# A graph layer on one core: one group in three, not one in four, sends all five of its windows through picked sets

## The chip, the cores and the metric

The kernel runs on one core of a Trainium2 chip. The metric is the device time of one execution in microseconds (us), as the median of several runs. The kernel before takes 1719.61 us (three runs, 1719.46 to 1721.19).

## The reference

A graph network layer with two edge types, a residual and a layer norm: 12500 nodes of 128 features, 400000 edges sorted by target node.

```python
src, dst = (edge_index[0], edge_index[1])
Xs = X[src]
m_data = Xs @ W_data.T + b_data
m_ctrl = Xs @ W_control.T + b_control
msg = jnp.where((edge_types == 0)[:, None], m_data, m_ctrl)
agg = jax.ops.segment_sum(msg, dst, num_segments=X.shape[0])
out = agg + (X @ W_self.T + b_self)
return jax.nn.relu(out)
...
x = _layernorm(x + _L0_gnn_ref(...), axis=-1)
```

## The kernel before

**Groups, windows and chunks.** The edges are cut into 3125 chunks of 128, and these into 25 groups of 125. A group is five windows of 25 chunks. Because the edges are sorted by target, a window's edges go to a short run of nodes; a group has accumulators `acc` (feature by node, one for each edge type) and `cnt` (edge counts for the biases). Messages are summed before the weights are applied: the kernel adds up rows of x per target and type, and multiplies by W once per node when a group is finished.

x is held as three bf16 parts whose sum is the float32 number, 384 columns a row: in SBUF as `x3` (row n at block n // 128, lane n % 128), and in DRAM as `rows3`.

**Two ways for an edge to reach its source row.** A *gathered chunk* is an indirect DMA issued by POOL (`fetch`, L825): 128 rows of `rows3` arrive as the tile msg. PE then adds them into the window's PSUM bank with three matmuls (`add_rows`, L757), against a one-hot matrix psel (`choose`, L845, built by `select` at L533) with a column for each target node and type. A window's psel covers all its 25 chunks however many are gathered.

A *picked set* takes 20 chunks of a window at once and without a DMA per chunk. DVE ranks the 2560 edges by the block and lane of their source row (L597 to L676: O, prod, found, rank, rm, rv), PE sorts them into 100 cells of 32 (`put`, L688), a 0.8 MB broadcast DMA on SP's queue brings the cells' lanes to all partitions (`spread`, L699 and L701), DVE makes them one-hot (`pick_matrix`, L743), PE picks the rows out of x3 (`pick`, L926, into PSUM tiles got), ACT copies them out as emsg (L940), and PE sums them into PSUM against a one-hot matrix esel (L533, L757). Edges that don't fit their cell go to 64 spare places; every second set one indirect DMA on POOL fetches these for two sets (`spare_rows`, L901, tile both). ACT copies half of it for the later set (L988, tile last), which waits for that DMA.

`sets(g)` says how many of a group's five windows have a picked set: all five if g is a multiple of 4, else four. A window with a set gathers its other 5 chunks (PB); the fifth window of the other groups gathers all 25 (PL). That is 7 x 5 + 18 x 4 = 107 sets and 7 x 25 + 18 x 45 = 985 gathered chunks.

**The order of work.** The main loop (L1177) runs over the sets. In the turn of set w there stand its picking and summing (five units of five cell columns each, `picked`), the ranking of sets w + 2 and w + 3, the pick matrix of w + 1, the chunks due in this turn, and the group work: `prep` of the next group (loading of edges, turning them, L494 to L522), `finish` and `pass_on` of a group whose windows are all closed. Gathered chunks are spread evenly over the turns from the third on, by `at = LAG + (n + ...) * (pairs - LAG) / total` (L1160). Their DMAs are paced (`paced`, L830): up to eleven places in a turn may each issue one, when it is due, 14 chunks (AHEAD) before the chunk that is due there, gated by a PE instruction of that place. A both gather takes the next such place, and POOL's queue is served in order. There are 18 msg buffers (HOLD).

`near_rows` (L460) works out, for all groups at once, where each chunk's window begins; its last instruction of three covers the groups with five sets by a stride of 4 (L469).

Of the kernel before, what the change touches and what calls it, by code (L numbers as in the profile page):

```python
# [31 lines left out]
NE = 5  # L32
NWIN = 2 * NE
LAG = 2
DPC = P * N // E
PAD = 10
PW = DPC + 2 * PAD
EW = 88
AW = PW + DPC * (PL - 1)
WMAX = max(AW, EW)  # L40
# [11 lines left out]
AHEAD = 14  # L52
FAR = -(-PW // DPC)
ACC_ROWS = 99 * P
# [101 lines left out]
def row_tables(nc, keep, tmp):  # L156
# [22 lines left out]
    for v in range(2):  # L179
# [4 lines left out]
        from_p = from_of[:, v, 0:1]  # L184
        nc.vector.tensor_scalar(from_p, k, float(DPC), float(-PAD), op0=OP.mult, op1=OP.add)
        nc.vector.tensor_scalar(from_e, from_p, -1.0, -1.0, op0=OP.mult, op1=OP.add)
# [20 lines left out]
def short_path(ctx, tc, const, ident, eps, wT, brow, bad, x, src, dst, etype, ws, bs, out):  # L207
# [12 lines left out]
    def side():  # L220

        return ps1.tile([P, 512], FP, name="side")

    def windows(g):

        c = g * GC
        for i in range(NE):
            yield "p", i, c, PB
            yield "e", i, c + PB, EC
            c += PB + EC  # L230

    def sets(g):

        return NE if g % 4 == 0 else NE - 1

    def of_p(g, i):

        return PL if sets(g) < NE and i == NE - 1 else PB

    each_e = [(g, i) for g in range(NG) for i in range(sets(g))]  # L240
    raw = {}

# [151 lines left out]
    for i, (_, _, c, _) in enumerate(windows(0)):  # L394
        nc.vector.memset(least[:, :, i:i + 1], float(max(0, c * DPC - PAD)))
    nc.vector.memset(x3[:, NBLK - 1], 0.0)
# [63 lines left out]
    def near_rows():  # L460

        first = pre.tile([GC, NG], FP, name="first", bufs=1)
        nc.vector.tensor_copy(first, first_all)
        ps = side()
        for v in range(3):
            nc.tensor.matmul(
                ps[:GC, v * P:v * P + NG], pick_first[:GC, v, :], first, start=True, stop=True, skip_group_check=True
            )
        for v, k, each in ((2, 0, 1), (1, 1, 1), (0, 1, 4)):  # L469
            start = from_of[:GC, v % 2, k:k + 1]  # L470
            nc.vector.tensor_scalar(
                near_all[:, k, ::each], ps[:GC, v * P:v * P + NG:each], start, None, op0=OP.add
            )

    def prep(g):

        s, d, t = raw.pop(g)
        v = 0 if sets(g) == NE else 1
        width = bounds_of[:GC, v, 0:1]
        sf = pre.tile([GC, P], FP, name="sf", bufs=1)  # L480
# [369 lines left out]
    def count(ps, sel):  # L850

        for r in range(FAR):
            n = len(range(r, CHUNKS, FAR))
            at = 2 * AW + DPC * r
            for t in range(2):
# [301 lines left out]
    for p in range(NG * NE):  # L1157
        run = gathered(*divmod(p, NE))
        for k, (_, u) in enumerate(run):
            at = LAG + (n + 0.9 - k / len(run)) * (pairs - LAG) / total  # L1160
            chunks.setdefault(int(at), []).append((at % 1, u))
# [3 lines left out]

    due[:] = [(LAG - 0.1) * (k + 0.5) / AHEAD for k in range(AHEAD)] + due[:-AHEAD]

# [9 lines left out]
    for w in range(pairs):  # L1177
        g, i = each_e[w]
        more = [(0.5, lambda: later(near_rows))] if w == 0 else []
        first = 1 if g == 0 else 0  # L1180
        if i == first and g + 1 < NG:
# [179 lines left out]
```

## Time and profile before

| what | value |
|---|---|
| median of three runs | 1719.61 us |
| profiled execution | 1721.01 us, span 1719.3 us |
| granted TensorE clock | 0.994 |
| PE busy in the span | 1568.1 us |
| DVE busy | 1529.0 us |
| ACT busy | 1243.3 us |
| POOL busy | 1286.8 us |
| first pick of set 0, pick of the last set | 58.3 us, 1679.9 us |
| bytes moved by DMA | 248.30 MB |

Busy time of an engine is the union of its instructions in the profile, without issuing and semaphore instructions; PE is matmuls, PEld the weight loads that overlap them. A group row of the profile reads: line, engine, operation, tiles out<-in, shapes, count | busy us, mean ns | idle time of that engine just before these instructions, and what ended it. A row of the timeline gives start and duration in us; in brackets stands the idle time before it and who ended it.

### The profile page before, as it was taken

How to read it: one execution, taken by the hardware profiler on the slowest of the kernel's cores; microseconds unless marked ns; L12 is line 12 of the kernel's file. 1: busy time of each engine (PE TensorE's matmuls, PEld its weight loads, DVE VectorE, ACT ScalarE, POOL GpSimd, SP SyncE). 2: the span in 40 equal slices, each digit the busy share in tenths (PEclk: the TensorE clock that was granted, in tenths of full speed). 3: DMA queues.
4: the chain of work that ended last, by engine and by line, in shares of the span. 5: the costliest groups of instructions: out<-in, count | busy, mean ns of one | idle time of the engine just before them, and what ended most of it. 6: DMA issues, size and time to landing. Idle time of an engine off the chain costs nothing.

```text
span 1719.3 us, 68641 instructions
## 1 busy us (share of the span) xinstructions
PE 1568.1 (91%) x28525; PEld 1241.5 (72%) x28525; DVE 1529.0 (89%) x3630; ACT 1243.3 (72%) x2198; POOL 1286.8 (75%) x1061
## 2 busy tenths in 40 slices
PE   0599999999999999999899999999999999999997
PEld 0377777777777777777677777777777777777776
DVE  6899899998998989999799899999999899999983
ACT  5777677776777667777576777676777676777675
POOL 0288878888788888888788777777788787777872
PEclk9999999999999999999999999999999999999999
DMA  7844454545444454444445554545544445544442
GB/s 195 280 149 133 126 160 124 147 147 152 134 139 142 139 148 135 140 150 129 144 122 150 160 155 136 152 130 152 150 144 138 135 128 159 155 140 129 138 128 59
DMA packets 148973, 248.30 MB, mean 144 GB/s; under 512 B 35937, under 2 KB 115260, under 8 KB 148652
## 3 DMA queue, kind: packets, MB, share of 16 engines
q1 hardware_dynamic: 85994, 134.45, 23.6%
q0 software_dynamic: 50032, 102.98, 22.2%
q10 hardware_dynamic: 12626, 6.40, 1.4%
q8 instruction: 225, 3.69, 0.9%
q14 instruction: 96, 0.79, 0.1%
HBM read 226.24 MB, written 17.50 MB: 142 GB/s over the span
## 4 chain that ended last, share of the span: by engine, by line
DVE 40%; PE 38%; issue 8%; ACT 5%; DMA 4%; DVEq 1%; POOL 0%; SPq 0%; ACTq 0%; POOLq 0%
PE sums L757 16%; PE got L926 12%; DVE esel L533 5%; DVE prod L641 5%; DVE prod L636 4%; DVE rv L676 3%; DVE pick L743 3%; DVE found L643 3%; PE side L1045 3%; ACT emsg L940 2%; DVE prod L614 2%; PE side L624 2%; DMA both<-rows,idx 2%; DVE psel L533 2%; PE side L688 2%
## 5 line engine op out<-in xcount | busy, mean ns | idle before, releaser
L825 POOL DMA_INDIRECT msg<-rows,idx_g x985 | 1215.5, 1234 | 309.7 <-issue 143.8
L940 ACT CAST emsg<-got 128x768 bf16<-128x768 f32 (+1 forms) x1070 | 949.0, 931 | 296.9 <-PE got L926 277.8
L757 PE MATMUL sums<-esel,emsg 128*128 128x176 bf16 x7704 | 686.6, 240 | 3.4 <-DVE acc L814 2.9
L757 PEld LDWEIGHTS <-emsg 128*128 128x128 bf16 x7704 | 569.5, 98 | 106.1 <-issue 98.8
L926 PE MATMUL got<-x,pick 128*32 128x384 bf16 x10486 | 569.1, 330 | 17.9 <-ACT emsg L940 8.8
L926 PEld LDWEIGHTS <-pick 128*32 128x32 bf16 x10486 | 240.4, 96 | 143.8 <-issue 19.9
L533 DVE TENSOR_TENSOR esel<-code_col,code 128x1760 bf16<-128x1760 bf16 x321 | 292.9, 913 | 11.8 <-PE sums L757 8.8
L757 PE MATMUL sums<-psel,msg 128*128 128x48 bf16 x2955 | 167.2, 184 | 11.8 <-DVE acc L814 9.0
L757 PEld LDWEIGHTS <-msg 128*128 128x128 bf16 x2955 | 138.6, 97 | 21.2 <-issue 16.4
L641 DVE TENSOR_TENSOR prod<-prod 128x1200 bf16<-128x1200 bf16 x214 | 134.0, 626 | 7.2 <-issue 1.1
L533 DVE TENSOR_TENSOR O<-cell_col,blk 128x2000 bf16<-128x2000 bf16 x107 | 128.0, 1197 | 7.1 <-ACT blk L439 4.3
L636 DVE TENSOR_TENSOR prod<-O,ahead 128x2000 bf16<-128x2000 bf16 x107 | 128.3, 1200 | 4.5 <-DVE ahead L632 1.9
L743 DVE TENSOR_SCALAR pick<-pick,lane_f 128x3200 bf16<-128x3200 bf16 x107 | 112.9, 1055 | 0.1
L901 POOL DMA_INDIRECT both<-rows,idx x54 | 66.2, 1226 | 54.4 <-ACT emsg L940 41.8
L688 PE MATMUL side<-rv,O 128*128 128x64 bf16 x2140 | 83.4, 195 | 25.0 <-DVE rv L676 22.1
L533 DVE TENSOR_TENSOR psel<-near_col,near 128x1200 bf16<-128x1200 bf16 x125 | 96.7, 773 | 9.7 <-issue 8.7
L814 DVE TENSOR_TENSOR acc<-acc,sums 128x176 f32 (+2 forms) x232 | 66.8, 288 | 42.1 <-PE sums L757 41.3
L688 PEld LDWEIGHTS <-O 128*128 128x128 bf16 x2140 | 79.0, 100 | 27.2 <-DVE rv L676 22.3
L676 DVE TENSOR_TENSOR rv<-rm,vals 128x1280 bf16<-128x1280 bf16 x107 | 87.9, 822 | 3.3 <-DVE key L649 1.4
L643 DVE TENSOR_REDUCE found<-prod 128x20 f32<-128x600 bf16 x107 | 82.9, 775 | 3.2 <-DVE prod L641 0.4
L614 DVE TENSOR_TENSOR prod<-O 128x1000 bf16<-128x1000 bf16 x107 | 72.0, 673 | 0.0
L624 PEld LDWEIGHTS <-ltri 128*128 128x128 bf16 x1284 | 40.4, 96 | 40.0 <-issue 38.5
(196 smaller groups left out, 1544.6 us busy)
## 6 DMA issues: line engine op xcount, KB each, us to landing
pick<-there SPq DMA_DIRECT2D x106, 800.0 KB
msg<-rows,idx_g POOLq DMA_INDIRECT x985
acc<-acc_start SPq DMA_DIRECT2D x23, 640.0 KB
rows<-x SPq DMA_DIRECT2D x6, 1344.0 KB
xs<-in_x_dram SPq DMA_DIRECT2D x99, 62.5 KB
out_dram<-h SPq DMA_DIRECT2D x99, 62.5 KB
xt<-in_x_dram ACTq DMA_DIRECT2D x6, 896.0 KB
cnt<-cnt_start SPq DMA_DIRECT2D x22, 160.0 KB
```

The lines of the kernel that those rows point to most:

```text
L533: nc.vector.tensor_tensor(sel.rearrange("p n (w t) -> p n w t", t=2), col[:rows].rearrange("p (o w t) -> p o w t", o=1, t=2).to_broadcast( ...
L614: nc.vector.tensor_add(h[:, :2 * CQ], s["O"][:, :2 * CQ], s["O"][:, 2 * CQ:])
L636: nc.vector.tensor_tensor(prod[:, :, :NCELL], s["O"], ahead.rearrange("p (o j) -> p o j", o=1).to_broadcast([P, EC, NCELL]), op=OP.mult,)
L641: nc.vector.tensor_add(prod[:, :, :h], prod[:, :, :h], prod[:, :, h:2 * h])
L643: nc.vector.tensor_reduce(found, prod[:, :, :h], AX.X, OP.add)
L676: placed[:] = [nc.vector.tensor_tensor(rv.rearrange("p c v (r t) -> p c v r t", t=2), rm.rearrange("p c (o r t) -> p c o r t", o=1, t=2).t ...
L688: nc.tensor.matmul(s["rk"][:m, :2 * CAP], s["held"][:, c * NCELL:c * NCELL + m], s["rv"][:, c].rearrange("p v r -> p (v r)"), start=(c == ...
L743: nc.vector.tensor_scalar(t, t, lane_f, None, op0=OP.is_equal)
L757: last = nc.tensor.matmul(out, msg[:, j * D:(j + 1) * D], sel, start=(start and j == 0), stop=stop, skip_group_check=True)
L825: return nc.gpsimd.indirect_dma_start(out=msg, out_offset=None, in_=rows3[:, :], in_offset=bass.IndirectOffsetOnAxis(ap=codes["p", g][0][: ...
L926: last = nc.tensor.matmul(ps[CAP * a:CAP * (a + 1), :], slots[w]["pick"][:, a * NQ + q, :], x3[:, 4 * q + a - a0].rearrange("p j d -> p (j ...
L940: s["out"] = nc.scalar.copy(msg[:, :n], ps[:, :n, :3 * D])
```

## The change

A constant EACH = 3 takes the place of the 4, in `sets` and in the stride of `near_rows`. Groups 0, 3, 6, ..., 24 now have five sets: 9 x 5 + 16 x 4 = 109 sets, and 9 x 25 + 16 x 45 = 945 gathered chunks.

```diff
@@ -32,6 +32,7 @@
 NE = 5
 NWIN = 2 * NE
 LAG = 2
+EACH = 3
@@ -231,7 +232,7 @@
     def sets(g):
 
-        return NE if g % 4 == 0 else NE - 1
+        return NE if g % EACH == 0 else NE - 1
@@ -466,7 +467,7 @@
-        for v, k, each in ((2, 0, 1), (1, 1, 1), (0, 1, 4)):
+        for v, k, each in ((2, 0, 1), (1, 1, 1), (0, 1, EACH)):
             start = from_of[:GC, v % 2, k:k + 1]
             nc.vector.tensor_scalar(
                 near_all[:, k, ::each], ps[:GC, v * P:v * P + NG:each], start, None, op0=OP.add
```

All line numbers of the kernel after are one higher. POOL's queue, its first gathers of the main loop, before:

```order
L901 DMA both<-rows_115,idx 128x384
L825 DMA msg<-rows_115,idx_g 128x384 x17
L901 DMA both<-rows_115,idx 128x384
L825 DMA msg<-rows_115,idx_g 128x384 x18
L901 DMA both<-rows_115,idx 128x384
L825 DMA msg<-rows_115,idx_g 128x384 x19
```

The same places of the queue after (L902 is `spare_rows`, L826 is `fetch`; from one both to the next are two sets):

```order
L902 DMA both<-rows_115,idx 128x384
L826 DMA msg<-rows_115,idx_g 128x384 x16
L902 DMA both<-rows_115,idx 128x384
L826 DMA msg<-rows_115,idx_g 128x384 x18
L902 DMA both<-rows_115,idx 128x384
L826 DMA msg<-rows_115,idx_g 128x384 x18
```

Behind each both stands about one gather fewer, all through the program: 18 or 19 (20 at five places) before, 17 or 18 (19 at three) after.

DVE in the turn of set 17, which before is the first set of group 4, from the rank of set 19 on:

```order
L645 CAST rank<-found 128x40
L533 TENSOR_TENSOR rm<-rank_col,rank 128x640
L533 TENSOR_TENSOR esel<-code_col,code 128x1056
L676 TENSOR_TENSOR rv<-rm,vals_5777 128x1280
L494 TENSOR_SCALAR rel<-dsts,near_all 125x128 x2
L495 TENSOR_SCALAR kind_r<-typs 125x128
L499 TENSOR_TENSOR worst<-worst,rel 125x256
```

And after, where set 17 is the fifth set of group 3:

```order
L646 CAST rank<-found 128x40
L534 TENSOR_TENSOR rm<-rank_col,rank 128x640
L650 SCALAR_TENSOR_TENSOR key<-rank,pk 128x20
L677 TENSOR_TENSOR rv<-rm,vals_5747 128x1280
L615 TENSOR_TENSOR prod<-O 128x10x100
L605 TENSOR_TENSOR prod<-blk_6207,blk_184 128x20x20
```

A set more stands ahead of the preparation of group 5 (rel, kind_r, worst), which has moved to the next turn; the ranking of a set is the same run of instructions in both.

## Prediction

> **What bounds the kernel now.** First the page's busy line, then the groups of GpSimd.
>
> ```profile
> PE 1568.1 (91%) x28525; PEld 1241.5 (72%) x28525; DVE 1529.0 (89%) x3630; ACT 1243.3 (72%) x2198; POOL 1286.8 (75%) x1061
> ...
> L825 POOL DMA_INDIRECT msg<-rows,idx_g x985 | 1215.5, 1234 | 309.7 <-issue 143.8 <-PE got L926 61.5 <-PE sums L757 56.0
> ...
> L901 POOL DMA_INDIRECT both<-rows,idx x54 | 66.2, 1226 | 54.4 <-ACT emsg L940 41.8
> ```
>
> PE and DVE look like the bound, and POOL looks like an engine with a quarter to spare. The instructions of the tile msg (minimum, median and maximum in ns, first and last start; below, POOL's idle time by what ended it) say otherwise:
>
> ```profile
> L825 POOL DMA_INDIRECT msg<-rows,idx_g x985: 940/1092/4512, 77.5 to 1686.3; - x197
> ...
>   issue: 160.2, 503
>   PE got L926: 61.5, 179
>   PE sums L757: 56.0, 179
> ```
>
> Each gap is a constant: 160.2/503 = 0.32 us, 61.5/179 = 0.34, 56.0/179 = 0.31. POOL hardly ever waits for anything; it pays about 0.31 us to get from one gather to the next. So a gather occupies POOL for (1215.5 + 309.7)/985 = 1.55 us, and 985 of them, with 54 of the both gathers at about 1.53 us (1.226 and the same gap), make 1608 us, against 1686.3 - 77.5 = 1609 us from the first to the last gather. POOL's queue has no slack.
>
> That alone doesn't make POOL the bound, since gathers are paced up to 14 chunks ahead of their use. The place where it hurts shows in the timeline:
>
> ```profile
> 188.84 0.29 ACT L581 ACTIVATE idx<-part 128x1 int32<-128x1 f32 x1
> ...
> 198.25 1.67 POOL L901 DMA_INDIRECT both<-rows,idx  x1 [0.30 <-DMA msg<-rows,idx_g]
> ...
> 202.17 0.51 ACT L988 COPY last<-both 64x384 bf16<-64x384 bf16 x1 [4.09 <-DMA both<-rows,idx]
> 202.58 0.20 ACT L696 CAST cell<-side 128x64 bf16<-128x64 f32 x1
> ...
> 202.84 0.21 PE L709 MATMUL side<-ident_b,cell 128*32 128x25 bf16 x4 [3.48 <-ACT cell L696]
> ```
>
> The indices of a both gather were ready at 189.13, but it stood behind queued msg gathers until 198.25. ACT, in order, waited 4.09 us for its rows, and with ACT's next copy PE stood for 3.48 us. In the list of waits, and for two long stretches by themselves (the first row of the three is the whole run, the second the stretch 196.7 to 945.3, the third what ended idle time before the tile both's instructions in 945.3 to 1656.6):
>
> ```profile
> ACT last L988 <- DMA both<-rows,idx: 29.0, 16, 7.1
> ```
> ```profile
> ACT last L988 <- DMA both<-rows,idx: 22.2, 13, 7.1
> ```
> ```profile
>   DMA both<-rows,idx: 4.0, 1
> ```
>
> The two stretches, all engines, and then the picks (L743, one for each set) alone:
>
> ```profile
> core 0: us, PE busy (x) PEld busy (x) DVE busy (x) ACT busy (x) POOL busy (x), PEclk, DMA share, GB/s
> 196.70:945.30 748.60, 702.62 (x12810) 557.63 (x12810) 672.98 (x1571) 538.10 (x971) 600.24 (x477) 0.99 0.47 141
> 945.30:1656.60 711.30, 679.43 (x12521) 539.92 (x12519) 652.68 (x1520) 527.82 (x944) 558.95 (x464) 1.00 0.48 144
> ```
> ```profile
> 196.70:945.30 748.60, 50.76 (x48) 0.99 0.47 141
> 945.30:1656.60 711.30, 49.54 (x47) 1.00 0.48 144
> ```
>
> A set takes 15.60 us in the first, 15.13 in the second. With 0.305 us behind each of its 477 and 464 instructions POOL is taken to 99.6% and 98.5%. In the second stretch PE is busy for 95.5% and DVE for 91.8%, and only one both gather comes late. So PE and DVE together set the pace, and a full POOL queue adds stalls on top. The change moves work from the second kind of cost to the first.
>
> **The change, part by part.** Two sets are added. In the quiet stretch, less its one wait of 4.0, a set's time is (711.3 - 4.0)/47 = 15.05 us, which holds also the gathered chunks and the groups' work. Their PE rows there (msg by the tile, with PE, PEld and POOL; then three rows of the groups' work):
>
> ```profile
> 945.30:1656.60 711.30, 75.06 (x1329) 62.27 (x1329) 529.80 (x441) 1.00 0.48 144
> ```
> ```profile
> L856 PE MATMUL sums<-psel,one_col 128*32 128x96 bf16 (+1 forms) x636 | 25.1, 208 | 0.0
> L1045 PE MATMUL side<-wT,acc 128*125 128x128 f32 x160 | 24.0, 273 | 0.0
> ...
> L1045 PE MATMUL side<-wT,xT 128*125 128x128 f32 x80 | 18.2, 309 | 0.8
> ```
>
> Chunks take 75.06/47 = 1.60 us of a set's time, counting and finishing 67.3/47 = 1.43. A set by itself is 15.05 - 1.60 - 1.43 = 12.0 us, two are **+24.0**. Between what ends? With the 0.68 us in which PE idles per set filled, 11.3 each; if the set waits on DVE alone, so that chunks hide and nothing is taken off for them, 15.05 - 1.43 = 13.6. I take 12.0, the value of the stretch itself. The two sets' other parts (a 0.8 MB broadcast each on SP's queue, one more both gather, ten ACT copies each) lie beside this: ACT was busy for 527.82 of 711.3 and DMA for 0.48.
>
> Forty gathered chunks go. On PE a chunk is 75.06/443 (1329 matmuls, three each) = 0.17 us, together **-6.8**; if DVE is what is waited for, nothing. The one-hot psel of a window is built for all 25 of its chunks whichever path they take, so DVE saves nothing there. Counting stays whole too. Edits to the two indexing strides cost nothing that differs: the same three instructions write 9 columns instead of 7.
>
> On POOL 40 gathers go and one both comes: -40 x 1.55 + 1.53 = -60 us. Per set that is (945 x 1.55 + 55 x 1.53)/107 = 14.5 us where 15.3 stood, against the 15.0 that PE and DVE need: 96% taken, with 0.5 us a set to work a backlog off. What that buys is only the waits behind the queue. What is an ACT wait worth on PE's path? 3.48/4.09 = 0.85 at 202; the two stretches differ by 0.47 x 48 = 22 us, of which the first has two finished groups more (rows below, 50.6 against 42.2 us, so 8.4), and 14 us stand against 18.2 us more waiting, 0.77. With 0.85, 29.0 us are worth 24.7. At 98.5% taken 4.0 us were left of 22.2, so at 96% I take nine tenths as gone: **-22.2**. Bounds: nothing gone, or all 29.0.
>
> ```profile
> L1045 PE MATMUL side<-wT,acc 128*125 128x128 f32 x192 | 28.8, 273 | 0.0
> ...
> L1045 PE MATMUL side<-wT,xT 128*125 128x128 f32 x96 | 21.8, 308 | 1.0
> ```
>
> What is late next when those stalls go: PE's short waits for DVE and ACT within each set, which 12.0 includes. Sum: +24.0 - 6.8 - 22.2 = -5.0. The profiled execution took 1721.0 us (span 1719.3 and 1.7 around it), so 1716.0; the median of the runs is 1.4 lower than it, so **1714.6, said as 1715**.
>
> **Rivals.** *Even trade.* The price of the sets at 20 and a relief of 20 cancel: 1719.6. Two terms of one size with opposite signs make this the nearest neighbour of the forecast. Nothing within 0.2% (3.4 us) can be told from no change.
>
> *The backlog stays, slower.* Gathers are stretched by DVE, as here, where one took 4.51 us (940 ns is the least):
>
> ```profile
> 559.93 4.51 POOL L825 DMA_INDIRECT msg<-rows,idx_g  x1 [0.30 <-issue]
> 559.94 1.18 DVE L533 TENSOR_TENSOR O<-cell_col,blk 128x2000 bf16<-128x2000 bf16 x1
> ...
> 561.05 1.19 DVE L636 TENSOR_TENSOR prod<-O,ahead 128x2000 bf16<-128x2000 bf16 x1
> ...
> 562.16 0.77 DVE L533 TENSOR_TENSOR psel<-near_col,near 128x1200 bf16<-128x1200 bf16 x1
> ...
> 562.85 1.28 DVE L641 TENSOR_TENSOR prod<-prod 128x1200 bf16<-128x1200 bf16 x2
> ...
> 564.34 0.78 DVE L643 TENSOR_REDUCE found<-prod 128x20 f32<-128x600 bf16 x1 [0.21 <-DVE prod L641]
> ```
>
> Two more sets bring more DVE instructions of this kind. The stretch is 1.234 - 0.940 = 0.29 us a gather, 290 us in all, 2.7 us a set. If it belongs to the set, it falls on 8.8 instead of 9.4 gathers: 1.247 us each. POOL stays full from the point at which 17.7 gathers and one both fill two sets' 30.0 us: a mean of (30.0 - 1.53)/17.7 - 0.305 = 1.30 us. Then only some 5 us of waiting go, and +17.2 - 5 = +12 gives 1732; with the sets at 13.6 and no relief from chunks, +27 - 5, it is 1741. Against it stands that 1.247 is short of 1.30. The Trainium skill's page "SBUF — State Buffer", section "Who interferes with whom", says that a tensor_tensor takes only the shared read interface and infers that it does not hold up descriptor generation, while a tensor_scalar in a two-port mode blocks GpSimd for its whole length. By that rule only the pick of a set (1.06 us, 50.76/48) and small ones count against the change. The 4.51 us gather lay beside a run of tensor_tensors with no tensor_scalar among them, so this trace speaks against the inference.
>
> *POOL is the clock.* If PE's 91% are not PE at its peak and POOL's gapless queue alone sets the end, the time falls with it. With the stretch kept to the sets: -40 x (0.940 + 0.31) + 2 x 2.7 + 1.2 = -43, so 1676. Against it: the second stretch ran 3% faster per set than the first with the same POOL queue, and -43 would ask for 14.6 us a set from a PE that now leaves 0.68 of 15.13 idle. The Trainium skill, "Trainium Kernel Development and Optimization", section "Performance Expectations", calls matmul busy time a bad metric, because matmuls are pipelined, and weight loads' busy share a good one. By that rule PE, with loads at 72%, has room and this rival gains. The rows of stalls, where PE stands idle for an ACT that waits, are too few to carry 43 us.
>
> *The change does not do what it says* can be left out: the written order has 945 and 55 gathers.
>
> **How the numbers follow.** Forecast, 1700 to 1716: 0.42. Even trade, within 3.4 us of 1719.6: 0.21. Backlog stays or sets dearer, 1723 to 1745: 0.30. POOL the clock: 0.07. So faster 0.49, same 0.21, slower 0.30. The bounds of the terms, -13 to +27 about the median, are 1706 to 1747; I leave out POOL the clock and the dearest end of the slower case, and give **1700 to 1738**.
>
> **What would show it.** Right: ACT's waiting for the both gathers falls from 29.0 to under 6 us; POOL's gaps grow beyond 0.31 us in many places, with "PE got" and "PE sums" as real releasers; a set takes about 15.0 us throughout, with PE busy for some 95% of it; PE's busy time rises by about 17 us. Wrong: the mean gather grows beyond 1.30 us and the waits stay (the backlog), or PE's idle time falls far below 0.6 us a set and the time drops by over 20 us (POOL the clock), or a set costs 15 us with the stalls gone (DVE is waited for more than the rows of PE show).

## The result, and the profile after

The kernel after takes 1713.19 us (median of six runs, 1710.92 to 1714.54) against 1719.53 us for the kernel before (six runs, 1718.26 to 1724.21): 6.3 us less, ratio 0.9958 with a 95% interval of 0.9944 to 0.9971. The profiled execution took 1713.78 us, its span is 1712.1 us.

The page's busy line and the two groups of POOL, in the same columns as before (all lines of the kernel are one higher):

```profile
PE 1579.8 (92%) x28838; PEld 1256.1 (73%) x28838; DVE 1550.1 (91%) x3676; ACT 1261.5 (74%) x2230; POOL 1255.6 (73%) x1022
...
L826 POOL DMA_INDIRECT msg<-rows,idx_g x945 | 1186.6, 1256 | 320.8 <-issue 139.0
...
L902 POOL DMA_INDIRECT both<-rows,idx x55 | 63.9, 1162 | 67.4 <-DMA xs<-in_x_dram 26.2
```

PE and DVE are busy for longer, 11.7 and 21.1 us, and yet the run is shorter. What went is idle time. Of the instructions of the tile both, the row on what ended idle time before them:

```profile
  DMA both<-rows,idx: 3.2, 3
```

That was 29.0 us in 16 places. The waits of POOL for its gates, from the list of waits (total, times, longest), show why:

```profile
POOL msg L826 <- PE got L927: 87.1, 206, 2.7
POOL msg L826 <- PE sums L758: 58.8, 165, 1.8
```

The mean gap behind "PE got" is now 0.42 us and the longest 2.7, against 0.34 and 1.7 before: in more places than before POOL reaches a gather ahead of its gate, where it mostly arrived late, with the bare 0.31. The both gather that the prediction followed, in the timeline of the kernel after (start, duration, idle time before and who ended it):

```profile
187.97 0.29 ACT L582 ACTIVATE idx<-part 128x1 int32<-128x1 f32 x1
...
190.13 1.24 POOL L902 DMA_INDIRECT both<-rows,idx  x1 [0.87 <-ACT emsg L941]
...
197.03 0.51 ACT L989 COPY last<-both 64x384 bf16<-64x384 bf16 x1
```

Its indices are ready at 188.26 and it starts at 190.13, after a gap of 0.87 us, in which POOL truly waited (an emsg copy of ACT ended the wait); before, it stood in the queue for 9.1 us. When ACT comes to the copy at 197.03, the rows are there, and no bracket stands behind it. In the chain of work that ended last, by engine, DMA's 4% of the kernel before are 1% now; first before, then after:

```profile
DVE 40%; PE 38%; issue 8%; ACT 5%; DMA 4%; DVEq 1%; POOL 0%; SPq 0%; ACTq 0%; POOLq 0%
```
```profile
PE 42%; DVE 39%; issue 7%; ACT 7%; DVEq 1%; DMA 1%; ACTq 0%
```

Two long stretches again, all engines, and then the picks alone:

```profile
195.80:933.40 737.60, 707.31 (x12966) 564.68 (x12965) 681.10 (x1589) 547.63 (x985) 573.34 (x457) 1.00 0.47 141
933.40:1649.50 716.10, 688.07 (x12694) 547.64 (x12692) 665.92 (x1548) 536.24 (x962) 561.74 (x447) 1.00 0.47 142
```
```profile
195.80:933.40 737.60, 51.57 (x49) 1.00 0.47 141
933.40:1649.50 716.10, 50.68 (x48) 1.00 0.47 142
```

A set takes 15.05 us in the first and 14.92 in the second, where 15.60 and 15.13 stood, and PE is busy for 95.9% and 96.1%. The slow first stretch of the kernel before is gone.

### The profile page after: what moved, and what is told of

Its sections match the earlier page's. It is cut to its first block, busy times and chain, and to the rows that moved or that the text cites. A ratio compares the mean times of both kernels' runs of the same rounds, so it can differ in the third digit from the quotient of the medians.

```text
span 1712.1 us, 69325 instructions
## 1 busy us (share of the span) xinstructions
PE 1579.8 (92%) x28838; PEld 1256.1 (73%) x28838; DVE 1550.1 (91%) x3676; ACT 1261.5 (74%) x2230; POOL 1255.6 (73%) x1022
## 4 chain that ended last, share of the span: by engine, by line
PE 42%; DVE 39%; issue 7%; ACT 7%; DVEq 1%; DMA 1%; ACTq 0%
PE sums L758 17%; PE got L927 14%; DVE prod L642 5%; DVE esel L534 4%; DVE prod L637 4%; ACT emsg L941 4%; DVE rv L677 3%; PE side L1046 3%; DVE pick L744 3%; DVE found L644 3%; DVE prod L615 2%; PE side L625 2%; PE side L689 2%; DVE psel L534 1%; DVE ahead L633 1%
## 5 line engine op out<-in xcount | busy, mean ns | idle before, releaser
L826 POOL DMA_INDIRECT msg<-rows,idx_g x945 | 1186.6, 1256 | 320.8 <-issue 139.0
L941 ACT CAST emsg<-got 128x768 bf16<-128x768 f32 x1090 | 965.8, 930 | 293.7 <-PE got L927 278.8
L758 PE MATMUL sums<-esel,emsg 128*128 128x176 bf16 x7848 | 695.4, 240 | 2.0 <-DVE acc L815 1.4
L758 PEld LDWEIGHTS <-emsg 128*128 128x128 bf16 x7848 | 577.8, 98 | 111.2 <-issue 104.0
L927 PE MATMUL got<-x,pick 128*32 128x384 bf16 x10682 | 577.2, 329 | 16.2 <-ACT emsg L941 9.1
L927 PEld LDWEIGHTS <-pick 128*32 128x32 bf16 x10682 | 246.5, 96 | 142.2 <-issue 19.3
L534 DVE TENSOR_TENSOR esel<-code_col,code 128x1760 bf16<-128x1760 bf16 x327 | 297.9, 911 | 7.5 <-PE sums L758 5.9
L758 PE MATMUL sums<-psel,msg 128*128 128x48 bf16 x2835 | 161.4, 184 | 14.8 <-DVE acc L815 11.8
L758 PEld LDWEIGHTS <-msg 128*128 128x128 bf16 x2835 | 134.2, 97 | 22.2 <-issue 19.8
L902 POOL DMA_INDIRECT both<-rows,idx x55 | 63.9, 1162 | 67.4 <-DMA xs<-in_x_dram 26.2
L633 DVE TENSOR_REDUCE ahead<-side 128x100 bf16<-128x200 f32 x109 | 39.5, 362 | 35.2 <-PE side L625 34.2
```

Of the source, the lines that this page charges most:

```text
L534: nc.vector.tensor_tensor(sel.rearrange("p n (w t) -> p n w t", t=2), col[:rows].rearrange("p (o w t) -> p o w t", o=1, t=2).to_broadcast( ...
L758: last = nc.tensor.matmul(out, msg[:, j * D:(j + 1) * D], sel, start=(start and j == 0), stop=stop, skip_group_check=True)
L826: return nc.gpsimd.indirect_dma_start(out=msg, out_offset=None, in_=rows3[:, :], in_offset=bass.IndirectOffsetOnAxis(ap=codes["p", g][0][: ...
L927: last = nc.tensor.matmul(ps[CAP * a:CAP * (a + 1), :], slots[w]["pick"][:, a * NQ + q, :], x3[:, 4 * q + a - a0].rearrange("p j d -> p (j ...
L941: s["out"] = nc.scalar.copy(msg[:, :n], ps[:, :n, :3 * D])
```

## The experiments

Kernels that were run together ran on one chip, beside the kernel before on that same chip; each ratio is to the latter. Gains and losses in whole microseconds are worked out from the ratio and 1720 us; the medians differ from them by up to 2 us. The "theory of two terms" in the expectations is the prediction: a price of some 17 us and a relief of some 22 us.

**The relief without the price (skip40).**

```diff
+        if k % 24 == 12 and k < 24 * 40:
+            fetched.append(last_msg[0])
+            return None
-        msg = mp.tile([P, 3 * D], BF, name="msg")
+        msg = last_msg[0] = mp.tile([P, 3 * D], BF, name="msg")
```

> The kernel before (one group in four), with 40 of its 985 gathers left out: each of these chunks adds the rows of the chunk ahead of it once more, so PE, DVE and ACT have the same work and POOL has 40 gathers less (part of the computation is changed). Theory of two terms: the relief of the change without its price. ACT's wait for the both gathers falls from 29 us to under 5, and the time by about 22 us, to 1697 (1693 to 1703). Rival, POOL is the clock: the time falls by POOL's 40 x 1.25 to 1.55 us, to 1657 to 1670. Rival, the gain comes from the order of the sets and not from the queue: no change, 1716 to 1722.

1695.04 us, ratio 0.9859 (0.9834 to 0.9884), 24 us off (1.4% of 1720). Its page's busy line, and what ACT's copy waited for:

```profile
PE 1560.5 (92%) x28525; PEld 1236.5 (73%) x28525; DVE 1528.7 (90%) x3630; ACT 1243.1 (73%) x2198; POOL 1238.6 (73%) x1021
```
```profile
ACT last L995 <- DMA both<-rows,idx: 5.5, 6, 1.8
```

DVE's and ACT's busy times are those of the kernel before to within 0.3 us; the waits went and the time with them. PE's busy time fell by 7.6 us, with the same 28525 matmuls; where that comes from stands with the account of the prediction below. Neither the order of the sets nor POOL as a clock (1657 to 1670) gives this.

**The price without the relief (extra40).**

```diff
+        if k % 23 == 12 and k < 23 * 40:
+            more = mp.tile([P, 3 * D], BF, name="more", bufs=2)
+            nc.gpsimd.indirect_dma_start(out=more, ...)
         return nc.gpsimd.indirect_dma_start(
             out=msg, out_offset=None, in_=rows3[:, :],
```

> The kernel after (one group in three), with 40 gathers more, whose rows nobody reads, so that POOL has 985 of them again (spread evenly, each ahead of a gather of the kernel). Theory of two terms: the price of the change without its relief. The waits for the both gathers come back to 20 us or more, and the time is about 17 us above the kernel before, 1737 (1730 to 1742). Rival, POOL is the clock: as the kernel before, 1718 to 1722. Rival, order of the sets: as the kernel after, 1711 to 1716.

1732.91 us, ratio 1.0069 (1.0044 to 1.0094): 12 us slower than the kernel before and 19 slower than the kernel after, whose sets it has. The waits are back:

```profile
ACT last L997 <- DMA both<-rows,idx: 26.4, 10, 6.4
```

The median lies in the range that was given, at its lower part. The sign of the change hangs on POOL's 40 gathers and the transfers that go with them.

**The wait alone (nowait4 and nowait3).** The same edit on both kernels:

```diff
-                    nc.scalar.copy(slots[w]["last"][:OVF, :], slots[w]["both"][:OVF, :])
+                    nc.scalar.copy(slots[w]["last"][:OVF, :], x3[:OVF, 0].rearrange("p j d -> p (j d)"))
```

> The kernel before, with ACT's copy from both to last reading constant rows of x3 in place of the gathered ones (the spare rows of every second set are left out of the sums). POOL's queue is as before, only ACT does not wait for it there. Theory of two terms: the waits behind the queue are what was gained, so the time falls by 15 to 25 us, to 1695 to 1705, with POOL still without gaps. Rival, POOL is the clock: no change, 1717 to 1722, since PE comes to wait for msg instead. Rival, order of the sets: no change.

> The kernel after, with the same edit to ACT's copy (the spare rows of every second set are left out). Theory of two terms: only 3.2 us of this wait are left in the kernel after, so 1709 to 1714, a change of at most 4 us from it, against 15 to 25 us for the same edit on the kernel before. Rival, order of the sets: the edit is worth the same on both kernels.

On the kernel before: 1702.00 us, ratio 0.9903 (0.9879 to 0.9927), 17 us off. On the kernel after: 1712.24 us, 0.9958 (0.9941 to 0.9975), the ratio that it has without the edit. So this one wait carries most of the relief, and in the kernel after no gain from it is left that the runs can tell. In nowait4 every gap of POOL behind "PE got" and "PE sums" is at most 0.3 us, so the queue is full, and its gathers take 1588 us from the first to the last (77.2 to 1665.6) where the kernel before takes 1609: the queue of the kernel before had some 20 us to give. PE waits more for msg than in the kernel before (8.2 us before weight loads against 3.0), which fits the smaller gain than in skip40:

```profile
PEld L757 <- DMA msg<-rows,idx_g: 8.2, 10, 2.0
...
PE sums L757 <- DMA msg<-rows,idx_g: 5.9, 7, 1.9
```

**Further along the same line (each2 and each6).**

```diff
-EACH = 3
+EACH = 2   # each2; 6 in each6
```

> One group in two has five sets: 113 sets and 865 gathered chunks, four sets more and 80 chunks fewer than the kernel after. Theory of two terms: nothing is left to relieve, so only the price is paid, twice that of the change, 2 x 17 to 18 us: 1747 to 1750. Rival, POOL is the clock: 2 x 43 to 60 us less than the kernel after, 1593 to 1627. Rival, a set costs its whole 15 us and a chunk nothing: 4 x 15 = 60 us more, 1773.

> One group in six has five sets (0, 6, 12, 18, 24): 105 sets and 1025 gathered chunks, two sets fewer and 40 chunks more than the kernel before. Theory of two terms: on this side of the kernel before POOL's queue, full already, becomes the clock: 1025 x 1.55 + 53 x 1.53 = 1670 us from its first to its last gather in place of 1609, or 43 us more if the stretch belongs to the sets, so 1763 to 1781. Rival, the waits only grow as they shrank from before to after: 17 us less for the sets and 22 us more waiting, 1725.

Both numbers were missed. each2 takes 1760.86 us, ratio 1.0234 (1.0204 to 1.0264), 47.7 us more than the kernel after and not 34 to 36. The busy line:

```profile
PE 1619.5 (92%) x29464; PEld 1281.7 (73%) x29464; DVE 1597.1 (91%) x3768; ACT 1303.0 (74%) x2294; POOL 1165.1 (66%) x944
```

Against the kernel after PE is busy for 39.7 us more and DVE for 47.0. The time follows DVE's number: four sets at 12.0 are 48.0, and the 80 chunks give nothing back. That lies between the prediction's price (34) and its dearer bound (13.6 a set and nothing back, 54), and nearer to the latter, in which chunks hide beside DVE's work; that DVE is the cause here was not tried by itself.

each6 takes 1739.34 us, ratio 1.0111 (1.0078 to 1.0144), 18 us slower than the kernel before by the medians, where 43 to 61 were expected. POOL is full there, and its gathers are shorter than in the kernel before. The group's row and the wait:

```profile
L826 POOL DMA_INDIRECT msg<-rows,idx_g x1025 | 1230.7, 1201 | 314.5 <-issue 149.6
```
```profile
ACT last L989 <- DMA both<-rows,idx: 64.6, 22, 8.4
```

A gather takes 1.201 us instead of 1.234, and 1025 x (1.201 + 0.307) and 53 x 1.5 make 1625 us, not 1670; the trace has 1622 from the first to the last gather, 13 more than before. Two accounts fit, and these rows do not part them. The waits grew by 35.6 us; at 1 us of time for each, less the 17 us of two sets, that is 18 us, which is what was measured (at the prediction's 0.85 it is 13). Or the full queue, with the gathers as they ran, set the pace: 13 to 17 us more.

**ACT's copy at another place (late4, late3, later4, later3, later4b).** The first two were meant to move the copy later, but left out the order that held it back:

```diff
-            if t == turns - 1 and "both" in slots[w]:
-                with tc.issue_after(s["out"].ins):
-                    nc.scalar.copy(slots[w]["last"][:OVF, :], slots[w]["both"][:OVF, :])
 ...
+            if late:
+                last, both = late.pop()
+                nc.scalar.copy(last[:OVF, :], both[:OVF, :])
             early, *more = tiled.get(turns, [lambda: None])
```

> The kernel before, whole, with ACT's copy from both to last moved from the end of a set's last unit into the first unit of the next set, behind that unit's own copies and just ahead of the sums that read it: the gather has some 2.5 us more to land, and the same instructions run. Theory of two terms: of the waits, what exceeds 2.5 us stays, some 8 of 29 us, so the time falls by 14 to 20 us, to 1700 to 1706, with POOL's queue as full as before and PE beginning to wait for msg in places. Rival, POOL is the clock: no change, 1717 to 1722.

> The kernel after with the same later copy. Theory of two terms: 3.2 us of this wait are left in the kernel after, so at most 3 us less, 1709 to 1714, and late4 comes out ahead of it by 5 us or more, since it does not pay for the two sets.

With nothing to hold it, the copy was put five instructions earlier on ACT, not later (ahead of four emsg copies and the cast into last): a wait made longer instead of shorter. late4 takes 1779.97 us, ratio 1.0343 (1.0316 to 1.0370), late3 1766.43 us, 1.0260 (1.0230 to 1.0291). In late4:

```profile
ACT last L994 <- DMA both<-rows,idx: 127.5, 53, 5.6
```

98.5 us more waiting cost 59 us. The expectations don't apply to these kernels as they came out, but they show the same wait at four times its size, at 0.6 us of time for each us of it. The granted clock is 0.981 in this profile, against 0.994 in the kernel before.

Then with the order set, behind two emsg copies of the next set:

```diff
+                with tc.issue_after(out.ins):
+                    nc.scalar.copy(last[:OVF, :], both[:OVF, :])
```

> The kernel before, whole, with ACT's copy from both to last really moved: an order is set that puts it behind the first two emsg copies of the next set, in place of ahead of them (the first try left out this order, and the copy came to stand five emsg copies earlier than in the kernel before). Theory of two terms: the gather has two copies, 0.8 and 1.1 us, more to land, with what PE does between them some 2.3 us; waits beyond that stay, about 8 of 29 us, so the time falls by 12 to 18 us, to 1702 to 1708. Rival, POOL is the clock: no change, 1717 to 1722.

> The kernel after with the same later copy. Theory of two terms: 3.2 us of the wait are left in the kernel after, so 0 to 3 us less, 1710 to 1713, and behind the kernel before with the same edit.

> The same kernel as later4 (the kernel before, whole, with ACT's copy behind the first two emsg copies of the next set), since its first run fell on a chip on which the kernel before itself took 2021 us, with PE pausing in hundreds of places and POOL's queue no longer full. Where the kernel before takes about 1720 us: theory of two terms, 12 to 18 us less, a ratio of 0.990 to 0.993, and ahead of the kernel after (0.996), with ACT's wait for the both gathers at 4 to 12 us of 29. Rival, POOL is the clock: no change, 0.998 to 1.002.

The first two, and skip40mm below, fell on a chip on which the kernel before itself takes 2021.08 us, with another bound: in later4's trace POOL waits 243.7 us for "PE got" and no wait for both is left in its list, so there is nothing for the theory to act on. later4 has 1.0040 (1.0017 to 1.0063) there, later3 0.9971 (0.9949 to 0.9992). Where the kernel before takes 1719.08 us, later4b takes 1728.41 us, ratio 1.0060 (1.0041 to 1.0078), slower and not faster. The wait for the DMA did go, but another came in its place. What ended idle time before the tile both's instructions in later4b, and then a row of its list of waits:

```profile
  DMA both<-rows,idx: 2.4, 1
```
```profile
PEld L757 <- ACT last L995: 28.6, 53, 3.1
```

```profile
883.83 0.51 ACT L995 COPY last<-both 64x384 bf16<-64x384 bf16 x1
...
884.40 0.19 PEld L757 LDWEIGHTS <-last 128*128 128x128 bf16 x3 [0.32 <-ACT last L995]
884.41 0.40 PE L757 MATMUL sums<-esel,last 128*128 128x176 bf16 x3
...
884.85 0.34 DVE L814 TENSOR_TENSOR acc<-acc,sums 128x176 f32 x1 [1.46 <-PE sums L757]
```

The rows of the timeline show the chain at one place: the copy ends at 884.34, PE's last sums of the set start right behind it, and DVE, which adds those sums up, has waited for 1.46 us. PE's weight loads wait for the copy in all 53 places. My expectation had counted the two emsg copies as room for the gather and not as a delay of the sums. The wait that came, 28.6 us, is about the size of the one that went, 29.0; why the kernel is 10 us slower and not level stays open.

**The price of a chunk (skip40mm).** Forty chunks, here from the middle of windows, lose their gathers and their matmuls too:

```diff
+            spared = s["msg"] is None
+            if not spared:
                 add_rows(rows, s["msg"], sel, c == 0, c == n - 1)
```

> The kernel before, with 40 gathered chunks left out whole: their gathers and also their three matmuls each (40 chunks from the middle of windows, evenly spread; those edges are missing from the sums). It differs from the run with only the gathers left out by 120 matmuls. Theory of two terms with chunks priced on PE: 40 x 0.17 = 6.8 us less than that run, 0.982 of the kernel before, about 1688. Rival, DVE is what is waited for and a chunk's matmuls lie beside its work: as that run, 0.986, about 1695.

0.9829 (0.9793 to 0.9864) on the chip of 2021 us, beside 0.9859 (0.9834 to 0.9884) for skip40 on another. The intervals overlap, and POOL's queue is not full on that chip. What a chunk's matmuls cost on the path stays open.

## Why the prediction was right

1715 was forecast, 1713.19 measured: -5.0 against the profiled execution was worked out, -6.3 came. The mechanism and both of its terms were found, but the small sum of two large terms came out closer than either term is known.

**POOL's queue has no slack** holds in the main: 40 gathers fewer are worth 24 us with the other engines' instructions unchanged (skip40), and 40 more undo the change (extra40). It was put too strongly, since "PE got" had gaps of up to 1.7 us and nowait4 runs the same gathers in 20 us less. **The relief, -22.2**: 24 us in skip40, 19 us from extra40 to the kernel after (ratios 1.0069 and 0.9958). ACT's wait fell to 3.2 us, within the "under 6" that was named. **Its worth, 0.85 us for each us of ACT's waiting**: nowait4 gained 17 us for 29.0, 0.6, but new waits of PE for msg took some of it; skip40 gained 24 for the 23.5 us that went, 1.0.

**The price, +17.2**: the kernel after and skip40 both have 945 gathers on POOL, and lie 0.9958 - 0.9859 = 0.0099 apart, 17 us; nowait3 and skip40, on one chip, lie 17.2 us apart. The split into +24.0 and -6.8 is not settled, and the price does not carry on: each2 looks like +24 a pair with nothing back.

**PE's busy time** rose by 11.7 us and not by 17. Against skip40 it is 19.3, and from nowait4 to nowait3, whose profiles both have a clock of 0.999, it is 16.9. So the trace of before holds some 8 us of "busy" that belongs to the stalls. The timeline of before, just behind the stall of the prediction and far from any, shows it:

```profile
202.98 2.38 PE L757 MATMUL sums<-esel,emsg 128*128 128x176 bf16 x15
...
563.18 1.31 PE L757 MATMUL sums<-esel,emsg 128*128 128x176 bf16 x15
```

Fifteen such matmuls take 1.31 us elsewhere, as the second row shows. The same two places, by stretch (length, PE busy and matmuls, granted clock, DMA share, GB/s):

```profile
202.80:205.60 2.80, 2.76 (x23) 0.50 0.30 75
563.10:564.50 1.40, 1.40 (x21) 1.00 0.00 0
```

The granted clock is half for some 3 us behind the stall. Between the first picks and the last, the trace of before has four such places, at 203, 421, 824 and 1343 us, behind waits of ACT for the both gathers of 4.09, 1.75, 7.06 and 4.05 us; skip40 and nowait4 have none. (Other such waits of up to 2.37 us have none behind them either. The kernel after has one at 502 us, behind its longest wait, 2.38 us, and another of some 7 us at its start, 64 to 72 us.) Four times some 3 us at half speed is an estimate of 6 of the 7.6 us. So a stall costs more than the idle time in front of it, and the prediction's 0.85, taken from idle times alone, left this part out. That the relief was still about 22 is in part luck.

**Backlog stays**: the mean gather grew to 1.256 us where 1.247 was worked out and 1.30 is the point from which the queue stays full. The direction was right, and the margin held; but the rule behind the 1.247, that the stretch belongs to the set, holds only while sets come at about the same pace: it gives the same 1.247 for late3, where the same sets and gathers are spread over 53 us more and the mean is 1.206. By what the Trainium skill's page "SBUF — State Buffer", section "Who interferes with whom", infers, a tensor_tensor should not have counted; the same section says that one with two SBUF inputs does contend with GpSimd's reads. Besides the gather of 4.51 us, nine more in the trace of before took over 2 us, up to 3.6, with only tensor_tensors and tensor_reduces of DVE beside them. That too speaks against the inference; what in the gather is held up no run here shows.

**POOL is the clock** falls with skip40, which stopped at 1695 with POOL no longer full, and with nowait4, which gained 17 us with all of POOL's gathers in place. each6 does not speak against it, as said there: on that side a full queue may well set the pace. The reading by the Trainium skill's page "Trainium Kernel Development and Optimization", section "Performance Expectations", that PE at 73% of weight loads has room, gains nothing by these runs and is not refuted by them: in the stretches after, PE was idle for 4%, but by matmul busy time, the measure that the section calls a bad one, and DVE for 7 to 8%, and what each added set cost in each2 follows DVE's busy time.

## What to carry to other kernels

An engine that only issues can be full at 75% busy: look at whether its gaps are all the same constant, not at its share. When a full queue and full compute engines stand side by side, moving work between them gains until the waits behind the queue are gone, and from there on it only pays; of the four spacings run here one group in three is the fastest, with one in four 6 us above it, one in six 26 and one in two 47.7. A stall of the matmul engine is worth reading together with the granted clock behind it. Before a wait is moved to a later place, ask what reads its result there.

## What the runs showed that was not expected

The time scatters where ACT's copy waits for the both gathers. Fifteen runs of the kernel before spread over 13 us (1711.5 to 1724.5) and six of extra40 over 12, but five runs of skip40 over 2.0 us and ten of nowait3 over 2.2 us on the same chip. late3, with POOL busy for only 68% but this wait made longer, spreads over 13 us too. The copy's wait is not all of it, since nowait4, without it but with a full queue, spreads over 8 us; the cause was not tried.

A gather's duration goes with the share of the span in which DVE is busy: 1.201 to 1.210 us at 86 to 88% (each6, late4, late3), 1.220 to 1.235 at 89 to 90%, 1.250 to 1.262 at 91% (nowait3, the kernel after, each2), with 0.94 us as the least; the chip of the last paragraph is left out of this. It does not go with the number of sets alone: late3 and the kernel after both have 109.

One chip ran the kernel before in 2021 us, 17% above the others, at a granted clock of 0.967 to 0.975 in the three kernels profiled there. Their instructions have the usual durations (got 0.336 us against 0.330 in later4b, esel 0.915 against 0.911), but PE stands still in hundreds of places before its weight loads with no releaser in the profile:

```profile
PEld L927 <- issue: 186.5, 351, 1.9
```

This row is later4's there; on the other chip the same kernel has 24.5 us in 67 places. What stops PE there stays open.
